# Attention and depthwise convolution on one core: groups of seven steps, one buffer for v, and most statistics of x taken during the first image

## The chip, the cores and the metric

The kernel runs on one core of a Trainium2 chip. The metric is device time in microseconds of one execution, as the median of several runs. The core has TensorE (matmuls, PE in the profile), VectorE (DVE), ScalarE (ACT), GpSimd (POOL) and the queue engine SP, which only issues DMAs here. DMAs are also issued from GpSimd's queue and, in the tail, from ScalarE's.

## The reference

x has 16 images of 384 channels on a 32 x 32 grid, all float32. Two residual layers follow each other:

```python
x = x + attention(_gn(x), w_qkv, w_proj, b_proj)   # 8 heads of 48, 1024 tokens per image
x = x + _dwconv(_gn(x), w_sym)                     # 7 x 7 per channel, padding 3

def _gn(v, G=32, eps=1e-5):      # mean and variance over 12 channels x 1024 points
    g = v.reshape(B_, G, C_ // G, H_, W_)
    ...
attn = softmax((q @ k.T) * 48 ** -0.5)
out = (attn @ v) @ w_proj.T + b_proj
w_sym = (weight + rot90(weight, 1) + rot90(weight, 2) + rot90(weight, 3)) * 0.25
```

## The kernel before

An image is three tiles of 128 channels x 1024 tokens. Its 8 heads are four units of two heads; a unit has two halves of 512 queries, and each half eight steps of 128 keys, so an image has 64 steps. A step is `s_step` (two score matmuls side by side into a PSUM buffer of two banks, L331, then the exp on ScalarE, L339) and `av_step` (the exponentials times v, L347, which also sums the softmax's denominators through a column of ones in v). The PSUM pool `ps_s` has three such buffers, which scores, q/k (`qk_step`, L280), v (`v_step`, L306) and projection (`proj_step`, L398) share; `ps_o` has two banks for the sums of AV. `take` (L358) copies a finished half to SBUF on ScalarE.

The division by the denominators goes through DRAM: `sums_out` (L365, L366) writes them and reads them back spread over partitions, `invert` (L372) takes the reciprocal on VectorE, writes it and reads it back broadcast, `divide` (L383) multiplies. After an image's fourth unit the projection follows, ScalarE adds the bias (L406) and a DMA on GpSimd's queue adds x (L407): this is x1.

Group norm statistics are `Stats`: `channels` (bn_stats on VectorE, L195), `gather` (through DRAM to 32 rows, GpSimd's queue), `groups` (L208 to L220: bn_aggr on VectorE, called mv; then on GpSimd one addition of eps, ve, L210, the power -1/2 and two small operations, L212 to L214; then two DMAs that spread scale and shift, sc, over the channels). Each image has them twice, for x and for x1. For the first image's x and the last image's x1 `groups_on_pe` does the same with small matmuls against masks (L236). `apply` normalizes: x on ScalarE (`x_apply`, L265), x1 into a tile xn on GpSimd (`conv_begin`, L261).

The convolution is 49 taps per tile on VectorE, each one instruction (`conv_tap`, L455) that reads xn and x1 and adds into x1. Three tiles are worked on in turn. Four of the 48 tiles, two of image 14 and two of image 15, are done by TensorE instead (`conv_on_pe`, L557), from shifted copies that go through DRAM; VectorE adds their sum (L570). The output leaves on GpSimd's queue (L465).

Each engine runs its own instructions in the order in which the program lists them. That order comes from a planner in the kernel: it keeps a `clock` for TensorE and a `vclock` for VectorE from cost constants (US_STEP 1.716, US_TURN 0.353 and so on). The main loop takes GS = 4 steps at a time: four S, four AV, then one `project` or some q/k and v chunks of the next image when `credit` allows, then `catch_up`, which lists VectorE's work (taps, and functions that fell due through `after`) until `vclock` reaches `clock`. `finish`, called within the loop, lets the reciprocal fall due 7 us after its call. x of the next image is loaded when the last v chunk is issued (`issue`, `begin_x`), into a single buffer. The last unit of the last image is divided without DRAM (`divide_at_once`, L418 to L421) and projected from four 128-row weight tiles (`proj_part`, L431), of which three fit in `wp`.

Of the kernel before, what the change touches and what calls it, by code (L numbers as in the profile page):

```python
# [16 lines left out]
P = 128  # L17
HEADS = 8
# [26 lines left out]
def kernel(  # L45
# [64 lines left out]
    def run(general):  # L110
        tag = "g" if general else "f"
        with ExitStack() as stack:
# [11 lines left out]
            epool = pool("epool", 6)  # L124
# [14 lines left out]
            PE_TILES = [(b, k) for b in (B - 2, B - 1) for k in PE_K]  # L139
# [25 lines left out]
            nc.sync.dma_start(wp, w_proj_t.rearrange("(k p) c -> p k c", p=P))  # L165
# [7 lines left out]
            vs = []  # L173
            for i in range(2):
                t = wpool.tile([P, NT, VW], F32, name=f"v_{i}")
                nc.gpsimd.memset(t, 1.0)
                vs.append(t)
# [4 lines left out]
            mhalf = wpool.tile([P, NK], F32, name="mhalf")  # L182
# [5 lines left out]
            class Stats:  # L188
# [35 lines left out]
                def groups_on_pe(self, masks):  # L224

                    st = small.tile([P, NK, 2], F32, tag="st", name=f"st_{self.name}")
                    for k in range(NK):
                        nc.vector.bn_aggr(st[:, k, :], self.bs[:, k, :])
                    ps = ps_o.tile([P, HALF], F32, tag="acc", name=f"ps_st_{self.name}")

                    def average(c0, src):
                        for mo in range(NK):
                            blocks = [n for n, b in enumerate(MASK_BLOCKS) if b[1] == mo]
                            for n in blocks:
                                ki = MASK_BLOCKS[n][0]
                                nc.tensor.matmul(  # L236
                                    ps[:, c0 + mo : c0 + mo + 1],
                                    lhsT=masks[:, n, :],
                                    rhs=src[:, ki : ki + 1],
                                    start=(n == blocks[0]),  # L240
                                    stop=(n == blocks[-1]),
                                )

                    mean = small.tile([P, NK], F32, tag="mn", name=f"mn_{self.name}")
                    nc.vector.tensor_copy(mean, st[:, :, 0])
                    average(0, mean)
                    d = small.tile([P, NK], F32, tag="d", name=f"d_{self.name}")
                    nc.vector.tensor_tensor(d, mean, ps[:, 0:NK], ALU.subtract)
                    nc.vector.tensor_tensor(d, d, d, ALU.mult)
                    nc.vector.tensor_tensor(d, d, st[:, :, 1], ALU.add)  # L250
                    average(NK, d)
                    nc.vector.tensor_scalar(d, ps[:, NK : 2 * NK], EPS, None, ALU.add)
                    self.sc = small.tile([P, NK, 2], F32, tag="sc", name=f"sc_{self.name}")
                    nc.gpsimd.tensor_tensor(self.sc[:, :, 0], d, mhalf, ALU.pow)
                    nc.vector.scalar_tensor_tensor(
                        self.sc[:, :, 1], ps[:, 0:NK], -1.0, self.sc[:, :, 0], ALU.mult, ALU.mult
                    )

                def apply(self, dst, src, k, engine=None):
                    if engine is not None:  # L260
                        engine.tensor_scalar(  # L261
                            dst, src, self.sc[:, k, 0:1], self.sc[:, k, 1:2], ALU.mult, ALU.add
                        )
                        return
                    nc.scalar.activation(  # L265
                        dst,
                        src,
                        AF.Identity,
                        bias=self.sc[:, k, 1:2],
                        scale=self.sc[:, k, 0:1],  # L270
                    )

# [28 lines left out]
            def v_step(b, t2):  # L301
# [11 lines left out]
                for j in range(2):  # L313
                    dst = vs[b % 2][:, 2 * t2 + j, 0 : HEADS * (D + 1)]
                    nc.scalar.copy(  # L315
                        dst.rearrange("p (h d) -> p h d", d=D + 1)[:, :, 0:D],
                        ps[:, j, 0:C].rearrange("p (h d) -> p h d", d=D),
                    )

            def v_of(u, i, j):  # L320
                b, p = divmod(u, NP)
                c = (2 * p + j) * (D + 1)
                return vs[b % 2][:, i, c : c + 64]
# [90 lines left out]

            def divide_at_once(u, h):
# [6 lines left out]

            late, pps = {}, {}
# [230 lines left out]
            clock, vclock = 0.0, 0.0  # L654
# [3 lines left out]
            GS = 4  # L658
# [11 lines left out]
            def us_tap(dy, dx):  # L670
                late_us = 0.06 if active[0][0] >= B - 2 else 0.0
                return ((H - abs(dy)) * (W - abs(dx)) + (130 if len(active) > 1 else 270)) / 940 + late_us
# [70 lines left out]
            def x1_groups(b, st):  # L743
                st.groups()
                after(9.0, 0.0, lambda: x1_chains(b, st))

            def x1_chains(b, st):
                on_pe = [t for t in PE_TILES if t[0] == b]
                for k in range(NK - 1, -1, -1):
                    tail = b == B - 1  # L750
                    conv_begin(st, b, k, (nc.gpsimd, None, nc.vector)[k] if tail else nc.gpsimd)
# [9 lines left out]
            def begin_x(b):  # L761
                load_x(b)
                after(10.0, 3.8, lambda: x_channels(b))
# [12 lines left out]
            def x_apply(b, st):  # L776
                for k in range(NK):
                    st.apply(xns[b][:, k, :], xns[b][:, k, :], k)
                ready[b] = now() + 6.0

            def finish(u):
                sums_out(u)
                if u < U - 1:
                    after(7.0, 0.3, lambda: finish2(u))
# [5 lines left out]
            def finish3(u):  # L790
                b, p = divmod(u, NP)
                divide(u)
                if p == NP - 1:
                    proj.append((now() + 4.0, b))

            def queue(b):
                chunks.extend(("qk", b, i) for i in range(4))
                chunks.extend(("v", b, i) for i in range(2))
                chunks.extend(("qk", b, i) for i in range(4, 6))
                chunks.extend(("v", b, i) for i in range(2, 4))  # L800
# [5 lines left out]
            st.groups_on_pe(masks_0.rearrange("p (b c) -> p b c", c=P))  # L806
# [5 lines left out]
            while chunks:  # L812
                issue(chunks.popleft())
            vclock = clock
# [41 lines left out]

            credit = 0.0
            for n0 in range(0, NS, GS):
                b, r = divmod(n0, PER_B)
# [5 lines left out]
                for n in range(n0, n0 + GS):  # L865
                    s_step(n)
                if n0 == NS - 2 * GS:
                    after(3.5, 4.2, lambda: None)
                    divide_at_once(U - 1, 0)
                if n0 == NS - GS:  # L870
                    for o in range(NK):
                        proj_part(B - 1, o, (0, 1))
                    clock += 2 * US_PROJ
                for n in range(n0, n0 + GS):
                    av_step(n)
                    u, h, i = n // (2 * NT), n // NT % 2, n % NT
                    if i == NT - 1:
                        take(u, h)
                        if h == 1:
                            finish(u)  # L880
                clock += GS * US_STEP + US_TURN

                credit = min(credit + 12.0 * GS / PER_B, 2.0)
                if proj and proj[0][0] <= clock:
                    project(proj.popleft()[1])
                elif credit >= 2:
                    while chunks and credit >= 1:
                        kind, cb, i = chunks[0]
                        first = {"qk": 2 * NT * (i // 2), "v": 0, "rest": 2 * NT * 3}[kind]
                        if ready.get(cb, 1e9) > clock or r + GS < first:  # L890
                            break
                        issue(chunks.popleft())
                        credit -= 1
                catch_up(clock)
                if b == 1 and r == 0:
                    conv_prepare()
                if b == B - 1:

                    if r == 4 * GS:
# [3 lines left out]
                    if r == 8 * GS:  # L903
                        w4 = w_proj_4.rearrange("(t p) c -> p t c", p=P)
                        nc.sync.dma_start(wp, w4[:, 0:NK])
                        nc.sync.dma_start(late["w3"], w4[:, NK])
                    if r == 6 * GS:
                        conv_matrices(1, flat2(qkpool.tile([P, 2, N], F32, tag="qk", name="mat_1")))
                    if r == 8 * GS:
# [3 lines left out]
                    if r >= 9 * GS and (b, 0) not in x1s and all(c[0] > b - 2 for c in active):  # L913
# [5 lines left out]
                    if r in (10 * GS, 12 * GS, 14 * GS):  # L919
                        loads(1)  # L920


            late["tail"] = True
            b = B - 1
            divide_at_once(U - 1, 1)
            for t in (NP - 2, NP - 1):
                for o in range(NK):
                    proj_part(b, o, (t,))
            clock += US_PROJ * 4 / 3 + 1.0
            st = Stats(f"x1_{b}")  # L930
            for o in range(NK):
                residual(b, o)
                st.channels(x1s[b, o], o)
            conv_piece()
            st.groups_on_pe(late["masks"])
            clock += 7.0
            x1_chains(b, st)
# [58 lines left out]
```

## Time and profile before

| what | us |
| --- | --- |
| median of 3 runs | 3024.63 (3024.15 to 3026.47) |
| the profiled execution | 3021.88 |
| its span | 3020.0 |
| TensorE busy in it | 2970.3 |
| VectorE busy in it | 2616.1 |
| ScalarE busy in it | 1298.7 |
| GpSimd busy in it | 728.3 |

The profile comes from one execution, and its span begins with the first recorded instruction and ends with the last one. The page gives busy time per engine, the span in 40 slices, the chain of work that ended last, and groups of instructions by line. Starts and durations of single instructions come from the timeline. An idle time in brackets stands before the instruction that it names, with what ended it. The ends of matmuls are modelled, so starts are the safer mark.

### The profile page before, as it was taken

Reading aid. Unit: us, or ns where it says so; the run is one execution under the profiler, and the core shown is the slowest. Engines: PE = TensorE matmul, PEld = TensorE weight load, DVE = VectorE, ACT = ScalarE, POOL = GpSimd, SP = SyncE. Lnnn points to the kernel's source line nnn. Section 1 sums busy time; section 2 is a strip of 40 time slices with the busy share of each in tenths; the row PEclk is TensorE's granted clock in tenths of the full one; section 3 lists DMA queues with packets and bytes.
Section 4 is the critical chain, followed back from the end, with each engine's and each line's share of the span. In section 5 each row is a group of like instructions: output and inputs, shape, how many; then the busy total and the mean of one; then the engine's idle time right before and its main releaser. Section 6 shows DMA issues by size and latency. Waiting matters only on the chain.

```text
span 3020.0 us, 30559 instructions
## 1 busy us (share of the span) xinstructions
PE 2970.3 (98%) x11658; PEld 1166.2 (39%) x11658; DVE 2616.1 (87%) x2553; ACT 1298.7 (43%) x1469; POOL 728.3 (24%) x426
## 2 busy tenths in 40 slices
PE   7999999999999999999999999999999999999978
PEld 4333343433334343343434334343433434333333
DVE  1101898997999999999999999999999999999788
ACT  1534535354453545435353453535445353544400
POOL 1021004020140604215060320505133060411500
PEclk9999999999999999999999999999999999999989
DMA  2113031121312112131211313122131312212234
GB/s 70 38 23 67 15 66 37 39 53 33 67 36 58 23 52 51 36 70 39 52 30 36 66 36 66 42 46 37 36 66 36 66 37 51 37 43 38 89 83 114
DMA packets 68332, 149.42 MB, mean 49 GB/s; under 512 B 30880, under 2 KB 33168, under 8 KB 66640
## 3 DMA queue, kind: packets, MB, share of 16 engines
q1 hardware_dynamic: 47536, 90.80, 12.2%
q0 software_dynamic: 18560, 52.31, 7.8%
q10 hardware_dynamic: 2080, 4.26, 0.6%
q8 instruction: 94, 1.54, 0.2%
q14 instruction: 62, 0.51, 0.1%
HBM read 99.35 MB, written 29.49 MB: 43 GB/s over the span
## 4 chain that ended last, share of the span: by engine, by line
PE 90%; DVE 5%; issue 3%; POOL 1%; DMA 1%; ACT 0%; POOLq 0%; SPq 0%; DVEq 0%
PE ps_s L331 29%; PE acc L347 29%; PE ps_qk L280 16%; PE ps_v L306 8%; PE ps_proj L398 8%; DVE x L455 4%; POOL ve_x L210 1%; DMA wc<-in_w_conv 0%; PE ps_st_x L236 0%; DVE bs_x L195 0%; DMA out<-x 0%; DVE x L570 0%; DMA sums<-sum 0%; DMA sum<-o 0%; DVE o L383 0%
## 5 line engine op out<-in xcount | busy, mean ns | idle before, releaser
L455 DVE SCALAR_TENSOR_TENSOR x<-xn,wsym,x 128x960 f32<-128x960 f32 (+9 forms) x2156 | 2379.2, 1175 | 19.5 <-POOL xn L261 17.6
L339 ACT ACTIVATE e<-ps_s 128x1024 f32<-128x1024 f32 x1024 | 967.0, 1030 | 395.0 <-PE ps_s L331 390.1
L331 PE MATMUL ps_s<-qk 48*128 48x512 f32 x4096 | 948.6, 602 | 2.2 <-ACT e L339 2.2
L347 PE MATMUL acc<-e,v 128*64 128x512 f32 x4096 | 935.4, 598 | 0.0
L331 PEld LDWEIGHTS ps_s<-qk 48*128 48x128 f32 x4096 | 373.1, 186 | 566.8 <-issue 430.6
L347 PEld LDWEIGHTS acc<-e,v 128*64 128x64 f32 x4096 | 271.5, 136 | 632.4 <-issue 561.0
L280 PE MATMUL ps_qk<-x,wqk 128*128 128x512 f32 x1152 | 506.8, 596 | 2.3 <-DVE x L261 2.3
L407 POOL DMA_DIRECT2D x<-in_x x45 | 39.6, 881 | 1414.8 <-ACT x L406 1414.8
L280 PEld LDWEIGHTS ps_qk<-x,wqk 128*128 128x128 f32 x1152 | 217.0, 190 | 284.9 <-issue 278.3
L210 POOL TENSOR_SCALAR ve_x<-mv_x 32x1 f32<-32x1 f32 x30 | 313.8, 10461 | 44.4 <-DVE mv_x L208 43.3
L287 ACT COPY qk<-ps_qk 128x1024 f32<-128x1024 f32 x96 | 97.2, 1012 | 463.4 <-PE ps_qk L280 463.4
L306 PE MATMUL ps_v<-wv,x 128*128 128x384 f32 x768 | 254.5, 488 | 0.0
L398 PE MATMUL ps_proj<-o,wp 128*128 128x512 f32 x540 | 235.7, 595 | 0.2 <-DVE bs_x L195 0.2
L358 ACT COPY o<-acc 128x512 f32<-128x512 f32 x128 | 75.1, 587 | 307.2 <-PE acc L347 307.2
L261 POOL TENSOR_SCALAR xn<-x,sc_x 128x1024 f32<-128x1024 f32 x46 | 198.0, 4309 | 33.5 <-DMA sc_x<-gr_x 33.1
L195 DVE BATCH_NORM_STATS2 bs_x<-x 128x6 f32<-128x512 f32 x192 | 120.2, 680 | 98.8 <-DMA x<-in_x 98.7
L306 PEld LDWEIGHTS ps_v<-wv,x 128*128 128x128 f32 x768 | 144.7, 190 | 113.6 <-issue 20.3
L372 DVE RECIPROCAL rec<-sums 128x16 f32<-128x16 f32 x63 | 15.8, 250 | 185.4 <-DMA sums<-sum 185.3
L398 PEld LDWEIGHTS ps_proj<-o,wp 128*128 128x128 f32 x540 | 101.4, 190 | 134.4 <-issue 131.4
L315 ACT COPY v<-ps_v 128x384 f32<-128x384 f32 x128 | 55.1, 483 | 196.9 <-PE ps_v L306 196.9
L406 ACT ACTIVATE x<-ps_proj,bp 128x1024 f32<-128x1024 f32 x45 | 50.1, 1114 | 192.6 <-PE ps_proj L398 175.0
L383 DVE TENSOR_TENSOR o<-o,inv 128x1024 f32<-128x1024 f32 x63 | 76.6, 1216 | 55.5 <-DMA inv<-inv 34.0
(70 smaller groups left out, 486.1 us busy)
## 6 DMA issues: line engine op xcount, KB each, us to landing
inv<-inv SPq DMA_DIRECT2D x126, 256.0 KB
x<-in_x SPq DMA_DIRECT2D x48, 512.0 KB
x<-in_x POOLq DMA_DIRECT2D x48, 512.0 KB, 5.5
out<-x POOLq DMA_DIRECT2D x48, 512.0 KB, 3.5
qk<-qk SPq DMA_DIRECT2D x96, 128.0 KB
sh<-xd SPq DMA_DIRECT2D x38, 160.0 KB
o<-o SPq DMA_DIRECT2D x90, 64.0 KB
sh<-xd ACTq DMA_DIRECT2D x26, 160.0 KB
```

The costliest lines, as they stand in the source:

```text
L195: nc.vector.bn_stats(self.bs[:, k, 6 * h : 6 * h + 6], src[:, h * HALF : (h + 1) * HALF])
L210: nc.gpsimd.tensor_scalar(ve, mv[:, 1:2], EPS, None, ALU.add)
L261: engine.tensor_scalar(dst, src, self.sc[:, k, 0:1], self.sc[:, k, 1:2], ALU.mult, ALU.add)
L280: nc.tensor.matmul(ps[:, h, :], lhsT=wqk[:, k, s, t, :], rhs=xns[b][:, k, h * HALF : (h + 1) * HALF], start=(k == 0), stop=(k == NK - 1),)
L287: nc.scalar.copy(halves(qks[u][:, s, :]), ps)
L306: nc.tensor.matmul(ps[:, j, 0:C], lhsT=xns[b][:, k, t * P : (t + 1) * P], rhs=wv[:, k, :], start=(k == 0), stop=(k == NK - 1),)
L331: nc.tensor.matmul(ps[:, j, :], lhsT=qks[u][r, 1, i * P : (i + 1) * P], rhs=qks[u][r, 0, h * HALF : (h + 1) * HALF], start=True, stop=True,)
L339: nc.scalar.activation(es[n], ps, AF.Exp, scale=SCALE)
L347: nc.tensor.matmul(accs[u, h][64 * j : 64 * j + 64, :], lhsT=v_of(u, i, j), rhs=e[:, j, :], start=(i == 0), stop=(i == NT - 1),)
L383: nc.vector.tensor_tensor(os_[u], os_[u], invs.pop(u), ALU.mult)
L398: nc.tensor.matmul(ps[:, h, :], lhsT=wp[:, t, o * P : (o + 1) * P], rhs=os_[NP * b + t][:, h * HALF : (h + 1) * HALF], start=(t == 0), sto ...
L455: nc.vector.scalar_tensor_tensor(acc, xn1s[b, k].rearrange("p (h w) -> p h w", w=W)[:, iy, ix], wsym[:, k, dy + PAD, dx + PAD : dx + PAD + 1],
```

## The change

- The main loop takes groups of 7 steps, eight times, and one of 8 (`SIZES`). Chunks, projection and `catch_up` now have a place after the scores of a group too (`other`). The pool of exponentials has 8 buffers, not 6.
- v has one buffer. Its four chunks stand after an image's first group of scores; q/k of the next image are issued during the image as before.
- The statistics of x of images 2 to 15 are taken during the first image: `stream_in` loads each tile once more (42 loads of 512 KB), `stream_stats` takes bn_stats, `stream_gather` and `stream_groups` do all groups at once, into `x_sc`. `x_apply` of these images falls due 14 us after the load of x is issued.
- The first image ends as the last one does (`fast_finish`, `fast_end`): last unit divided without DRAM, four weight tiles, statistics on TensorE. `wp` gets its usual content afterwards.
- `conv_begin` normalizes x1 of images 1 to 14 on ScalarE (engine None) instead of GpSimd; images 0 and 15 use one engine for each tile. It falls due 14 us after `groups`, not 9.
- The reciprocal falls due 9 us after the end of its group.
- Three conv tiles are on TensorE: one of image 14, two of image 15. The planner's price of a tap changes.

```diff
-            epool = pool("epool", 6)
+            epool = pool("epool", 8)
...
-            PE_TILES = [(b, k) for b in (B - 2, B - 1) for k in PE_K]
+            FAST = (0, B - 1)
+            PE_TILES = [(B - 2, PE_K[0])] + [(B - 1, k) for k in PE_K]
...
-            vs = []
-            for i in range(2):
-                t = wpool.tile([P, NT, VW], F32, name=f"v_{i}")
-                nc.gpsimd.memset(t, 1.0)
-                vs.append(t)
+            v = wpool.tile([P, NT, VW], F32, name="v")
+            nc.gpsimd.memset(v, 1.0)
+            x_sc = wpool.tile([P, B, NK, 2], F32, name="x_sc")
...
+            def stream_in(b, k):
+                if not many:
+                    many["bs"] = npool.tile([P, B - 2, NK, 12], F32, tag="xn1", name="bs_all")
+                many[b, k] = rpool.tile([P, N], F32, tag="x1", name=f"xs_{b}_{k}")
+                nc.gpsimd.dma_start(
+                    many[b, k], x[b, k * P : (k + 1) * P].rearrange("p h w -> p (h w)")
+                )
+
+            def stream_stats(b, k):
+                t = many.pop((b, k))
+                for h in range(2):
+                    nc.vector.bn_stats(
+                        many["bs"][:, b - 2, k, 6 * h : 6 * h + 6], t[:, h * HALF : (h + 1) * HALF]
+                    )
...
-            GS = 4
+
+            SIZES = [7] * 8 + [8]
...
-                after(9.0, 0.0, lambda: x1_chains(b, st))
+                after(14.0, 0.0, lambda: x1_chains(b, st))
...
-                    tail = b == B - 1
-                    conv_begin(st, b, k, (nc.gpsimd, None, nc.vector)[k] if tail else nc.gpsimd)
+                    conv_begin(st, b, k, (nc.gpsimd, None, nc.vector)[k] if b in (0, B - 1) else None)
...
-                after(10.0, 3.8, lambda: x_channels(b))
+                if b == 1:
+                    after(10.0, 3.8, lambda: x_channels(b))
+                else:
+                    after(14.0, 0.0, lambda: x_apply(b, None))
...
-                if u < U - 1:
-                    after(7.0, 0.3, lambda: finish2(u))
+                if u % NP < NP - 1 or u // NP not in FAST:
+                    waiting.add(u)
+                    after(9.0, 0.3, lambda: finish2(u))
...
+            def fast_finish(b):
+                nonlocal clock, vclock
+                late["tail"] = b == B - 1
+                proj_part(b, 0, (NP - 2,))
+                divide_at_once(NP * b + NP - 1, 1)
+                for o in range(1, NK):
+                    proj_part(b, o, (NP - 2,))
+                x1_stats[b] = Stats(f"x1_{b}")
+                for o in range(NK):
+                    proj_part(b, o, (NP - 1,))
+                    residual(b, o)
+                    x1_stats[b].channels(x1s[b, o], o)
...
-                for n in range(n0, n0 + GS):
+                for n in range(n0, n0 + size):
                     s_step(n)
...
+                clock += (size * US_STEP + US_TURN) / 2
+                if r == 0 and b - 1 == FAST[0]:
+                    fast_end(b - 1)
+                if r == 0:
+                    for i in range(NT // 2):
+                        issue(("v", b, i))
...
+                else:
+                    other(r + size)
...
-                clock += GS * US_STEP + US_TURN
+                clock += (size * US_STEP + US_TURN) / 2
+                if n0 // (2 * NT) < (n0 + size) // (2 * NT):
+                    finish((n0 + size) // (2 * NT) - 1)
```

## Prediction

> **What bounds the kernel now.** I read the page first: busy times, then the chain that ended last.
>
> ```profile
> PE 2970.3 (98%) x11658; PEld 1166.2 (39%) x11658; DVE 2616.1 (87%) x2553; ACT 1298.7 (43%) x1469; POOL 728.3 (24%) x426
> ...
> DVE  1101898997999999999999999999999999999788
> ...
> PE 90%; DVE 5%; issue 3%; POOL 1%; DMA 1%; ACT 0%; POOLq 0%; SPq 0%; DVEq 0%
> ```
>
> TensorE carries the end. VectorE is nearly idle for four slices (300 us) and full afterwards; ScalarE is never on the chain. Next the chain in order of time (start, us, what): one projection per image.
>
> ```profile
> 53.81 10.30 PE ps_qk L280 x24
> ...
> 1498.12 15.65 PE ps_proj L398 x36
> ...
> 1676.24 15.65 PE ps_proj L398 x36
> ```
>
> An image takes 178.12 us, without TensorE idling. 24 full matmul passes take 10.30, so 0.429 each; a step (scores S, then AV) is 16 passes that run in pairs, 8 x 0.429 = 3.43 per group of 4 on each side. The timeline of one group, TensorE and then ScalarE (start, us, engine, line):
>
> ```profile
> 1691.82 3.70 PE L331 MATMUL ps_s<-qk 48*128 48x512 f32 x16
> 1695.45 3.65 PE L347 MATMUL acc<-e,v 128*64 128x512 f32 x16
> 1699.04 3.70 PE L331 MATMUL ps_s<-qk 48*128 48x512 f32 x16
> ```
>
> ```profile
> 1691.93 1.11 ACT L406 ACTIVATE x<-ps_proj,bp 128x1024 f32<-128x1024 f32 x1 [4.04 <-PE ps_proj L398]
> 1693.06 3.77 ACT L339 ACTIVATE e<-ps_s 128x1024 f32<-128x1024 f32 x4
> ...
> 1700.27 3.77 ACT L339 ACTIVATE e<-ps_s 128x1024 f32<-128x1024 f32 x4 [3.44 <-PE ps_s L331]
> ```
>
> S to AV is 3.63, AV to S 3.59: a group costs 7.22, of which 7.22 - 6.87 = 0.355 is the turn. The first exp starts 1.24 after its group (1693.06 - 1691.82), right behind the projection's copy; four exps take 3.77, so 0.91 from start to start and 1.03 each.
>
> Where ScalarE normalizes x today, and what GpSimd's small operations wait for (ScalarE, GpSimd, VectorE):
>
> ```profile
> 1558.25 3.77 ACT L339 ACTIVATE e<-ps_s 128x1024 f32<-128x1024 f32 x4 [0.53 <-PE ps_s L331]
> 1561.88 3.52 ACT L265 ACTIVATE x<-x,sc_x 128x1024 f32<-128x1024 f32 x3
> 1565.47 3.77 ACT L339 ACTIVATE e<-ps_s 128x1024 f32<-128x1024 f32 x4
> ```
>
> ```profile
> 1539.46 19.98 POOL L210 TENSOR_SCALAR ve_x<-mv_x 32x1 f32<-32x1 f32 x1
> ...
> 1569.30 11.57 POOL L261 TENSOR_SCALAR xn<-x,sc_x 128x1024 f32<-128x1024 f32 x1 [1.58 <-DMA sc_x<-gr_x]
> ```
>
> ```profile
> 1560.84 0.25 DVE L372 RECIPROCAL rec<-sums 128x16 f32<-128x16 f32 x1 [1.48 <-DMA sums<-sum]
> ```
>
> The three x operations sit behind four exps, in the AV half, and the next exps start on time (1558.25 + 7.22 = 1565.47). The 32x1 operation on GpSimd lasts 19.98 us and ends at 1559.44, when VectorE falls idle (1559.36 to 1560.84). Last, the clock in the tail (stretch, PE busy, ..., PEclk):
>
> ```profile
> 2870.00:2876.00 6.00, 4.10 (x18) 1.16 (x14) 5.86 (x5) 0.58 (x1) 0.00 (x0) 1.00 1.04 235
> 2876.00:2880.00 4.00, 2.13 (x4) 0.83 (x3) 3.96 (x4) 0.00 (x0) 0.00 (x0) 0.61 0.30 66
> 2880.00:2884.00 4.00, 4.00 (x6) 1.59 (x5) 3.89 (x4) 0.00 (x0) 0.00 (x0) 0.53 0.00 0
> ```
>
> Two idle stretches of 1.90 and 1.87 us (TensorE's timeline, before 2875.34 and 2878.31) halve the clock for the busy stretch behind them: its matmuls follow each other at 0.853.
>
> **What the Trainium skill says.** "PSUM — Partial Sum Buffer", section "Engine vs sequencer instructions": ScalarE's queue is a strict FIFO. The trace agrees (the first exp waits for the 1.11 us copy). "SBUF — State Buffer", section "Who interferes with whom": a VectorE operation with two SBUF inputs contends with a GpSimd one that reads SBUF. Taps are such; the 19.98 us agree. "TensorE: Matmul & The Clock Gate", section "What's actually happening": half clock after an idle window of 3.4 us, full after a busy one. The trace is harsher: PEclk 0.53 after shorter idling.
>
> **The change part by part.** From the order in which the changed kernel's instructions stand on each engine.
>
> *Groups of seven.* 16 groups per image become 9: 7 x 0.355 = 2.49 less, and one insertion more (+0.2, as 10.50 against 10.30): 175.8 per image. Three PSUM buffers let S run 3 steps ahead of its exp. Step 7 begins at 5.25 and needs exp 4, done at 1.24 + 3 x 0.91 + 1.03 = 5.0: it just fits, if ScalarE is free at the start. v in one buffer moves 15.7 us of matmuls behind an image's first S: no cost, AV of the last image is over.
>
> *x normalized at another place.* For images 3 to 15 the three x operations stand on ScalarE behind the projection's third copy and before the next seven exps (13 times). The first exp then starts at 1.24 + 3.57 = 4.81; S step 4 waits until 5.9 instead of 2.67, the seventh is 3.4 late. +3.4 each, nothing hides it. TensorE idles 3.2 us: half clock costs 0 to 3.4 more; I take 1.4, since the idling may be cut by a window's edge.
>
> *xn moved from GpSimd to ScalarE* (images 1 to 13): three more operations behind a pair of q/k copies and before seven exps, the same +3.4 at least. They wait for GpSimd's statistics, which nobody but GpSimd waited for. Between VectorE's mv and the first tap of the new image stand 31 taps, two reciprocals and a divide, and no wait that could bring a gap: the sums are now asked for 9 us after the group instead of 7 after its start. So I take it that the 32x1 operation is released only when VectorE runs dry before that tap. Bounds: 0 (released at once) to the following walk. From the first exp after xn: S ends 4.7; AV 6.15, S 6.2, AV 6.15, S 6.2, q/k 10.5, AV 6.15, S8 7.05, AV8 7.0 = 60.1; S 6.2, v 15.8, AV, S, AV 18.5, projection 15.65 = 116.3. Third x1 in place +7.2 (copy 1.2, GpSimd's DMA 5.5), bn_stats 1.2, 13 taps 14.2, mv 0.7, 31 taps and the rest 34.3: 173.9. Then from the end of ve to sc 9.9 (1559.44 to 1569.30), 0.1, xn 3.6: 187.5; half clock after 6 us of idling 2.6 (0 to 3.4). Period **190.1** instead of 178.12, with TensorE alone at 186.6 inside it. Image 2 is spared (VectorE idle): 175.8 + 9.6. In image 15 xn stands in the AV half of group 6, 160.6 after the same mark, and waits longer: mv at 124.7 + 9 taps 9.7 + conv matrices 2.2 + 0.7 = 137.3; 23 taps, matrices, a divide and reciprocals 28.0; 11 taps 11.8, where VectorE runs dry, since the inverse that it needs next stands on SP's queue behind the store of xn; then 10.0 and 3.6: 190.7. The next exps were due at 166.5: +24.2, and 5 for two half clocks.
>
> *First image.* Projection over four tiles (+5.2), two ones-matmuls (2), a wait for the 3.35 us reciprocal (1), statistics on TensorE 5 (as 2911.57 to 2916.58) and half clock 2. 42 loads of 512 KB every 4 us and their bn_stats (1.29 a pair) lie in VectorE's idle slices, where the DMA engines are 1 to 3 tenths busy. On GpSimd's queue they stand ahead of image 1's own statistics, needed on ScalarE at about 146 and done by 112. That the scales of 14 images come late for image 2: 0 to 10, I take 0.
>
> *Three conv tiles.* TensorE's tail loses 94.8/4 = 23.7, but VectorE's grows: after the last statistics 119 taps stand where 73 stood, since image 14's two tiles start no earlier. Before: 2918.06 to 3009.39 = 91.3; 46 taps at 1.08 less one addition: **138**. VectorE then ends last, 47 us over before, and the 23.7 are worth nothing.
>
> **Sum.** First q/k at 23.7, +32.5; image 0: 113.0 (64 x 1.716 + 9 x 0.355) + v 15.7 + a pair of q/k 10.5 + projection of two units 10.5, of the others 10.3 and 3.0 for ones-matmuls and the reciprocal; four q/k 21: image 1 starts at 240.2. +113 + 7 + 15.7 + 31.8 = 407.7, image 2. First exp after its xn: +123.7 = 531.4. 12 x 190.1: 2812.6. Image 15: S8, AV8 and the partial projection end 47.6 after 190.7, +5: 3055.9. To the last statistics 24.6 (as before, without its wait), +138.9, +10.6 to the end: span 3230. The profiled execution took 3021.88 for a span of 3020.0, the median is 3024.63: +4.6, so **3235**.
>
> **Rivals.**
> B, GpSimd gets through in time (xn was once let in two taps after a divide; no ve was): period 175.8 + 2 x 4.8 = 185.4, image 15 without the wait: 2756 + 217 + 174 + 4.6 = **3151**.
> C, not slower: ScalarE's queue never reaches TensorE. Its place is the 27 lumps, its price 0 instead of 3.4 and more; it decides if the seven exps start within 0.2 us of before. For it: ScalarE is 43% busy and off the chain. Against it: FIFO and three PSUM buffers. 407.7 + 13 x 175.8 + 155 (image 15: 113 + v 15.7 + two projections 26.2) + 174 + 4.6 = **3027**, no change; somewhat below 3018 if VectorE, no longer disturbed by GpSimd's xn (taps of 1.95 us), runs the tail quicker.
> D, more stalls (late scales, 3.4 for each half clock): **3275**.
>
> **Numbers.** A 0.55, B 0.27, C 0.10, D 0.08. The range takes A, B and most of D: 3115 to 3275. 0.2% (6 us) is what a measurement of this kernel tells from no change: slower 0.91, same 0.04, faster 0.05, the last two out of C.
>
> **What would show it.** Projections 190 us apart from image 2 on (178.12 before, 175.8 under C); on L331 idle time put down to ACT, near 3 us behind the projection; ve of GpSimd 30 us long, ending where VectorE idles; PEclk below 9; a tail in which VectorE works 138 us. If S groups take 6.2 everywhere, the prediction is wrong at the lumps.

## The result and the profile after

The changed kernel takes 3249.73 us (median of 4 runs, 3246.39 to 3251.95), the kernel before 3025.55 beside it: a ratio of 1.074, 95% interval 1.0722 to 1.0759. The profiled execution has a span of 3247.2 us.

The page, read in the same order as before: busy times, VectorE and TensorE's clock in 40 slices, and the first line of the chain that ended last.

```profile
PE 2992.1 (92%) x11478; PEld 1198.7 (37%) x11478; DVE 2645.5 (81%) x2608; ACT 1336.4 (41%) x1509; POOL 646.6 (20%) x317
...
DVE  3438933889989888998888989888898988899688
...
PEclk9999999999999999999999999999999999999895
...
DVE 4%; issue 1%; POOL 0%; POOLq 0%
```

TensorE's share fell from 98% to 92%, so it now waits. The prediction's sign "PEclk below 9" hardly shows: the digits stay at 9 except in two of the last three slices, each an average over 81 us. The mean granted clock over the whole execution does show it, 0.954 against 0.994 before. The chain covers only 5% of the span: it begins at 3096.93 us, at the last statistics, and could not be followed back further. It shows who ended last, and nothing of where 224 us went. For that one compares periods and groups of instructions. Two groups say most (busy us, mean ns of one, then the idle time before them and its releaser):

```profile
L401 PE MATMUL ps_s<-qk 48*128 48x512 f32 x4096 | 988.9, 632 | 152.7 <-ACT e L409 152.7
L217 POOL TENSOR_SCALAR ve_x<-mv_x 32x1 f32<-32x1 f32 x15 | 446.5, 29766 | 151.6 <-DVE mv_x L215 151.6
```

The score matmuls S idle 152.7 us, all put down to the exps of ScalarE. An addition on 32 numbers takes GpSimd 29.8 us on average. Of its 15 executions 13 take 33.86 to 39.55 us and two, at 96.13 and 485.12, take 0.25; during the one at 485.12 VectorE has nothing to do. TensorE's timeline of one image in the middle shows where the waits stand (start, length, ..., in brackets the idle time before):

```profile
1595.93 15.72 PE L468 MATMUL ps_proj<-o,wp 128*128 128x512 f32 x36
1611.58 2.85 PE L401 MATMUL ps_s<-qk 48*128 48x512 f32 x12
1617.15 5.45 PE L401 MATMUL ps_s<-qk 48*128 48x512 f32 x16 [2.73 <-ACT e L409]
1622.53 10.57 PE L350 MATMUL ps_qk<-x,wqk 128*128 128x512 f32 x24
...
1674.43 2.85 PE L401 MATMUL ps_s<-qk 48*128 48x512 f32 x12
1685.03 6.15 PE L401 MATMUL ps_s<-qk 48*128 48x512 f32 x16 [7.76 <-ACT e L409]
1691.11 6.23 PE L417 MATMUL acc<-e,v 128*64 128x512 f32 x28
```

A group of seven score steps without a wait takes 6.21. The one behind the projection takes 1622.53 - 1611.58 = 10.95, the one behind the q/k pair 1691.11 - 1674.43 = 16.68. In both, three steps (12 matmuls) go through, as many as there are PSUM buffers, and the fourth waits for an exp. From this projection to the next, at 1787.00, lie 191.07 us: 175.85 (the period measured below, in a run without these waits) + 4.74 + 10.47, what the two groups take beyond 6.21. ScalarE in the same stretch:

```profile
1611.69 1.11 ACT L476 ACTIVATE x<-ps_proj,bp 128x1024 f32<-128x1024 f32 x1 [4.04 <-PE ps_proj L468]
1612.70 3.49 ACT L272 ACTIVATE x<-x,x_sc 128x1024 f32<-128x1024 f32 x3
1616.10 3.74 ACT L409 ACTIVATE e<-ps_s 128x1024 f32<-128x1024 f32 x4
...
1674.53 1.01 ACT L357 COPY qk<-ps_qk 128x1024 f32<-128x1024 f32 x1 [4.13 <-PE ps_qk L350]
1680.57 3.50 ACT L272 ACTIVATE xn<-x,sc_x 128x1024 f32<-128x1024 f32 x3 [5.03 <-DMA sc_x<-gr_x]
1683.98 2.82 ACT L409 ACTIVATE e<-ps_s 128x1024 f32<-128x1024 f32 x3
```

The first exp starts 4.52 after its scores where x stands in front, and 9.55 where xn does, since xn waits 5.03 more for its scales. What these wait for is on GpSimd, and what releases GpSimd is on VectorE (first GpSimd's timeline, then VectorE's):

```profile
1637.59 33.87 POOL L217 TENSOR_SCALAR ve_x<-mv_x 32x1 f32<-32x1 f32 x1 [10.46 <-DVE mv_x L215]
```

```profile
1669.37 2.00 DVE L524 SCALAR_TENSOR_TENSOR x<-xn,wsym,x 128x841 f32<-128x841 f32 x2
1684.11 3.67 DVE L524 SCALAR_TENSOR_TENSOR x<-xn,wsym,x 128x1024 f32<-128x1024 f32 x3 [12.74 <-ACT xn L272]
```

The addition ends at 1671.46, 0.1 after VectorE's last tap (1671.37), and VectorE then waits for the xn whose scales that addition held up. So the loop is closed. At the end, VectorE's timeline from the last image's normalization to its last taps:

```profile
3097.16 0.81 DVE L268 TENSOR_SCALAR xn<-x,sc_x 128x1024 f32<-128x1024 f32 x1
...
3173.26 63.01 DVE L524 SCALAR_TENSOR_TENSOR x<-xn,wsym,x 128x930 f32<-128x930 f32 x57
```

From 3097.16 to 3236.27 VectorE works 139.1 us, where it worked 91.3 before.

### The profile page after: what moved, and what is told of

Read it like the earlier page. It is cut to its first block, busy times and chain, and to the rows that moved or that the text cites. A ratio compares the mean times of both kernels' runs of the same rounds, so it can differ in the third digit from the quotient of the medians.

```text
span 3247.2 us, 30093 instructions
## 1 busy us (share of the span) xinstructions
PE 2992.1 (92%) x11478; PEld 1198.7 (37%) x11478; DVE 2645.5 (81%) x2608; ACT 1336.4 (41%) x1509; POOL 646.6 (20%) x317
## 3 DMA queue, kind: packets, MB, share of 16 engines
q1 hardware_dynamic: 46800, 88.82, 11.1%
## 5 line engine op out<-in xcount | busy, mean ns | idle before, releaser
L524 DVE SCALAR_TENSOR_TENSOR x<-xn,wsym,x 128x899 f32<-128x899 f32 (+9 forms) x2205 | 2402.4, 1166 | 165.3 <-ACT xn L272 163.9
L401 PE MATMUL ps_s<-qk 48*128 48x512 f32 x4096 | 988.9, 632 | 152.7 <-ACT e L409 152.7
L417 PE MATMUL acc<-e,v 128*64 128x512 f32 x4096 | 910.7, 596 | 0.0
L401 PEld LDWEIGHTS ps_s<-qk 48*128 48x128 f32 x4096 | 399.0, 197 | 733.3 <-ACT e L409 389.4
L417 PEld LDWEIGHTS acc<-e,v 128*64 128x64 f32 x4096 | 281.2, 137 | 609.4 <-issue 609.4
L217 POOL TENSOR_SCALAR ve_x<-mv_x 32x1 f32<-32x1 f32 x15 | 446.5, 29766 | 151.6 <-DVE mv_x L215 151.6
L468 PE MATMUL ps_proj<-o,wp 128*128 128x512 f32 x504 | 220.0, 595 | 0.0
L468 PEld LDWEIGHTS ps_proj<-o,wp 128*128 128x128 f32 x504 | 94.6, 190 | 125.2 <-issue 123.3
L385 ACT COPY v<-ps_v 128x384 f32<-128x384 f32 x128 | 55.1, 483 | 186.6 <-PE ps_v L376 186.6
L202 DVE BATCH_NORM_STATS2 bs_x<-x 128x6 f32<-128x512 f32 x108 | 69.2, 687 | 64.8 <-DMA x<-in_x 64.5
L272 ACT ACTIVATE xn<-x,sc_x 128x1024 f32<-128x1024 f32 x44 | 51.5, 1231 | 105.2 <-DMA sc_x<-gr_x 77.4
```

Source lines behind the costliest of these rows:

```text
L202: nc.vector.bn_stats(self.bs[:, k, 6 * h : 6 * h + 6], src[:, h * HALF : (h + 1) * HALF])
L217: nc.gpsimd.tensor_scalar(ve, mv[:, 1:2], EPS, None, ALU.add)
L401: nc.tensor.matmul(ps[:, j, :], lhsT=qks[u][r, 1, i * P : (i + 1) * P], rhs=qks[u][r, 0, h * HALF : (h + 1) * HALF], start=True, stop=True,)
L417: nc.tensor.matmul(accs[u, h][64 * j : 64 * j + 64, :], lhsT=v_of(u, i, j), rhs=e[:, j, :], start=(i == 0), stop=(i == NT - 1),)
L468: nc.tensor.matmul(ps[:, h, :], lhsT=wp[:, t, o * P : (o + 1) * P], rhs=os_[NP * b + t][:, h * HALF : (h + 1) * HALF], start=(t == 0), sto ...
L524: nc.vector.scalar_tensor_tensor(acc, xn1s[b, k].rearrange("p (h w) -> p h w", w=W)[:, iy, ix], wsym[:, k, dy + PAD, dx + PAD : dx + PAD + 1],
```

## The experiments

Each is the changed kernel with the edit shown; times are medians, and ratios are to the kernel before, run beside them. None leaves out any of the computation.

**Statistics without starvation, the order kept**

```diff
-                    nc.gpsimd.tensor_scalar(ve, mv[:, 1:2], EPS, None, ALU.add)
+                    nc.vector.tensor_scalar(ve, mv[:, 1:2], EPS, None, ALU.add)
...
-                    nc.gpsimd.tensor_tensor(af[:, 1:2], mv[:, 0:1], af[:, 0:1], ALU.mult)
-                    nc.gpsimd.tensor_scalar(af[:, 1:2], af[:, 1:2], -1.0, None, ALU.mult)
+                    nc.vector.scalar_tensor_tensor(
+                        af[:, 1:2], mv[:, 0:1], -1.0, af[:, 0:1], ALU.mult, ALU.mult
+                    )
```

> The changed kernel, where in the images without a wait of VectorE for statistics (the groups of one image) the variance + eps goes to VectorE, and behind GpSimd's power the product -mean*rstd too: VectorE has to wait for GpSimd here, so that the power runs in a gap of VectorE's, 34 us earlier than now. The order of everything else stays. Theory (GpSimd is starved by the taps until VectorE runs dry, the scales reach ScalarE late, and in a FIFO the seven exps wait behind them): the 34 us are gone, xn costs what a lump of 3.6 us costs in any case (4.75 as behind the projection), the period falls from 191 to about 185.4, image 15 loses its wait of 24 us and more; 3249.7 - 12 x 5.6 - 27 = about 3155 (3140 to 3170). Rival (the scales are late for another reason, such as the place where the statistics are asked for, and the 34 us only fill the wait): 3250, period 191.

Measured: 3153.05, ratio 1.0424 (1.0406 to 1.0442). From 453.53 to 2865.59, the starts of the projections of images 1 and 14, lie 13 periods of 185.5 each. The theory's 3155 and 185.4 hold: the lateness of the scales is worth 96.7 us.

**The same with the addition left on GpSimd**

Only the second half of the diff above.

> The changed kernel with variance + eps and the power left on GpSimd, as one edit only: the product -mean*rstd is taken on VectorE, which so waits for GpSimd right behind its mv. Nothing else on GpSimd or ScalarE changes. Theory (GpSimd's 32x1 operation is starved by VectorE's taps and runs at once where VectorE waits): the operation lasts under 1 us instead of 34, and the time falls as with the variance on VectorE, to about 3153 (3145 to 3165). Rival (the operation is long or late of itself on GpSimd, so that VectorE now waits for it too): 3250 or more, since VectorE's taps of 34 us then stand behind it.

Measured: 3156.41, ratio 1.0441 (1.0424 to 1.0459). The addition's group of instructions:

```profile
L217 POOL TENSOR_SCALAR ve_x<-mv_x 32x1 f32<-32x1 f32 x15 | 3.4, 226 | 153.9 <-DVE mv_x L215 153.9
```

The same instruction on the same engine takes 226 ns instead of 29766, because VectorE stands still beside it: in the image with the addition at 1603.03, VectorE waits 1.00 us for GpSimd before its product. The addition was starved, not slow: this run shows it.

**xn back on GpSimd, which is starved as it was**

```diff
-                    conv_begin(st, b, k, (nc.gpsimd, None, nc.vector)[k] if b in (0, B - 1) else None)
+                    conv_begin(st, b, k, (nc.gpsimd, None, nc.vector)[k] if b in (0, B - 1) else nc.gpsimd)
```

> The changed kernel with one part undone: xn of every image but the first and last is computed by GpSimd again, not by ScalarE; GpSimd's statistics are starved as before. Theory (the wait costs only because ScalarE's queue carries it to TensorE): the S groups behind the q/k pair take 6.2 again, only the lump of x behind the projection stays (4.75), the period is 175.8 + 4.8 = 180.6, image 15 loses its 24 us and more: 3249.7 - 12 x 10.4 - 27 = about 3098 (3085 to 3115). Rival (VectorE is then late: dry 10 us for the scales and 11.6 more for GpSimd's xn, and its divides stand behind the taps that wait): 155 busy + 22 dry is near the period already, TensorE then waits for the divides and the time stays above 3130.

Measured: 3122.36, ratio 1.032 (1.0303 to 1.0338), between the two. The addition still takes 29.8 us on average, yet S behind q/k takes 6.21 again: late scales cost TensorE through ScalarE's queue. The period is 181.4 rather than 180.6, since S behind the projection takes 11.85 to 12.38 in four of 13 images; in eight others it takes 10.9 to 11.1, in the first 9.36. The other miss is in the last image, in TensorE's timeline:

```profile
2935.66 3.78 PE L500 MATMUL ps_proj<-o,wp 128*128 128x512 f32 x4 [9.42 <-DVE o L453]
```

VectorE's divides are late there, and a further wait of 6.87 follows. These two waits (16.3) and 0.8 in each of 12 periods (9.6) are about the 24 us by which the theory missed. So the rival was right for the last image only.

**x alone moved into the AV half, statistics starved**

A function put in `mid` is called right after the scores of a group and behind their exps.

```diff
+            mid = deque()
...
-                    after(14.0, 0.0, lambda: x_apply(b, None))
+                    after(14.0, 0.0, lambda: mid.append(lambda: x_apply(b, None)))
...
+                    while mid:
+                        mid.popleft()()
```

> The changed kernel, GpSimd's starved statistics left as they are, and only x's three operations moved from before the seven exps into the AV half behind them. The order that is worked out from costs shifts with it: xn's three now stand behind a group's exps and a q/k pair, in the AV half as well, about 64 us of TensorE's work behind the projection, and 32 taps instead of 44 stand between the last x1 and the point where VectorE runs dry. Theory (starvation has no price of its own; what counts is when the scales come against where xn stands, and whether exps follow at once): xn is ready at 7.2 + 1.2 + 10.9 + 0.7 + 27 + 10 + 3.6 = 60.6 behind the projection, before the AV half ends at about 70; so no stall although the 32x1 operation still lasts 20 us and more: period near 175.9, and with 6 taps more in the tail and a possible wait in image 15 3020 to 3060, about 3035. Rival (each stall has its own price, and starvation keeps its own): 3249.7 - 13 x 4.75 = 3188, period 186.

Measured: 3277.58, ratio 1.0839 (1.0822 to 1.0855). Both missed. I had worked out the order of one image and taken it for all, but the planner's order repeats only after three images here: projections stand 175.9, 206.2 and 201.6 apart. xn on ScalarE in an image of the first kind and in one of the second:

```profile
1695.56 3.50 ACT L272 ACTIVATE xn<-x,sc_x 128x1024 f32<-128x1024 f32 x3 [0.36 <-DMA sc_x<-gr_x]
...
1878.94 3.50 ACT L272 ACTIVATE xn<-x,sc_x 128x1024 f32<-128x1024 f32 x3 [27.57 <-DMA sc_x<-gr_x]
```

GpSimd's addition in the same two:

```profile
1662.02 24.03 POOL L217 TENSOR_SCALAR ve_x<-mv_x 32x1 f32<-32x1 f32 x1 [17.66 <-DVE mv_x L215]
...
1827.33 43.66 POOL L217 TENSOR_SCALAR ve_x<-mv_x 32x1 f32<-32x1 f32 x1 [8.31 <-DVE mv_x L215]
```

In the first kind it goes as the theory had it: 24 us of starvation, no stall, a period of 175.87. In the two others xn stands some 20 us earlier against the projection, in front of seven exps, and that group of scores takes 36.6 and 31.9 instead of 6.2. An edit that took away a stall of 4.75 per image moved another instruction to a place where it costs 25 to 30.

**The same order, statistics not starved**

The first diff and the one above together.

> The kernel with x's three operations in the AV half (the one at 3277.6) with the one addition that VectorE takes variance + eps and the product, so that GpSimd isn't starved. The order is the same as there: in one image of three xn stands in the AV half, in the two others some 20 us earlier, behind an AV and before seven exps. Theory (a lump in front of exps costs 4.75, and the 25 to 30 us more that those images took were the wait for starved scales): xn there finds its scales, since they come some 27 to 30 us behind the projection and it stands 40 behind it; periods 175.9, 180.6, 180.6, and 3020 + 9 x 4.75 + 9 taps x 1.08 = about 3073 (3060 to 3085). Rival (xn's early place itself is what makes it wait, starved or not): still above 3200.

Measured: 3030.52, ratio 1.0021 (1.0014 to 1.0028). In this order starvation alone is worth 3277.6 - 3030.5 = 247 us. The rival is out, and the theory missed by 42.5: I had priced an xn before the exps at 4.75, and it costs 0.08 (that S group takes 6.29). With 0.08 in its place the theory's sum is 3030. ScalarE's timeline of it:

```profile
1915.08 3.50 ACT L273 ACTIVATE xn<-x,sc_x 128x1024 f32<-128x1024 f32 x3
1918.49 1.91 ACT L410 ACTIVATE e<-ps_s 128x1024 f32<-128x1024 f32 x2
```

Its scores begin at 1917.05. xn starts 2 us earlier, because no copy stands before it that has to wait until TensorE turns to the scores, and the first exp comes 1.44 after them. So, as far as these runs show, what three operations cost depends on what holds their start: the copy of a projection or of q/k, or a late scale.

**Both sets of three in the AV half, statistics not starved**

To the run before is added:

```diff
-                after(14.0, 0.0, lambda: x1_chains(b, st))
+                after(14.0, 0.0, lambda: mid.append(lambda: x1_chains(b, st)))
```

> The changed kernel with the statistics of an image on VectorE as in the run without starvation, and both sets of three ScalarE operations (x behind the projection, xn behind q/k) put behind the exps of an S group, into the AV half, where ScalarE is idle. All work is the same, and three conv tiles stay. Theory (a lump costs by its place, in front of seven exps): no S group above 6.3 behind the projection or q/k, period 175.8, and the late scales of image 2 stay (+9.6): about 3033 (3022 to 3045), which is where the changed kernel would have been without any stall of ScalarE's. Rival (groups of seven leave ScalarE too little room, exps late anyway, or VectorE's waits come to bind): period above 180, more than 3085.

Measured: 3020.04, ratio 0.9989 (0.998 to 0.9998). The scores' group, which had 152.7 us of idle time:

```profile
L402 PE MATMUL ps_s<-qk 48*128 48x512 f32 x4096 | 918.7, 597 | 0.5 <-ACT e L410 0.5
```

Projections stand 175.85 apart. The time is 2 us under the theory's range: the late scales of image 2, for which it kept 9.6, cost TensorE nothing once x stands in the AV half. Against 3153.05 the 27 sets of three are worth 133.0, or 4.9 on average. One of the 27 is image 2's x, whose S group there takes 13.65 (7.4 more than 6.21) because of the late scales.

**Four conv tiles, in the changed kernel and in the one without stalls**

```diff
-            PE_TILES = [(B - 2, PE_K[0])] + [(B - 1, k) for k in PE_K]
+            PE_TILES = [(b, k) for b in (B - 2, B - 1) for k in PE_K]
```

> The changed kernel with one part undone: four conv tiles on TensorE at the end, not three. Theory (VectorE ends last, its 119 taps behind the last statistics set the end): 46 taps of 1.08 less and one addition of 1.2 more, VectorE's tail 139 -> about 91, TensorE's tail 23.7 longer but still not behind it: about 3202 (3195 to 3210). Rival (TensorE's conv tail was the longer or close behind, so that its 23.7 come back): 3225 or more.

> The kernel without stalls of ScalarE (statistics on VectorE, both lumps in the AV half), with four conv tiles on TensorE as in the kernel before. Theory (the two cuts add up, since they lie one behind the other): 3020.0 - 45 taps x 1.08 + one addition = about 2973, or a little later where TensorE's conv tail (95 us from the statistics on) ends after VectorE's: 2970 to 2985, 1.3 to 1.8% under the kernel before. Rival (TensorE's tail then binds by its full 23.7): 2995 or more.

Measured: 3199.44, ratio 1.0582 (1.0565 to 1.06), and 2974.03, ratio 0.9834 (0.982 to 0.9847). Three tiles for four cost 50.3 us in one kernel and 46.0 in the other, and the 23.7 that they spare TensorE do not show. In the second kernel both engines end together (TensorE's last conv matmuls, then VectorE's last addition):

```profile
2912.46 46.70 PE L627 MATMUL ps_conv<-sh,mat 128*32 128x512 f32 x452
```

```profile
2959.35 1.22 DVE L640 TENSOR_TENSOR x<-ps_conv,x 128x1024 f32<-128x1024 f32 x1
```

TensorE is busy for 99% of this span. It is the fastest version of the study, 1.7% under the kernel before.

**Groups of four in that version**

```diff
-            SIZES = [7] * 8 + [8]
+            SIZES = [4] * 16
```

> The kernel without stalls and with four conv tiles on TensorE, but in 16 groups of four steps an image instead of 9 of seven and eight: what the longer groups alone are worth. Theory (each turn between S and AV costs 0.355, less one insertion): period 178.1 instead of 175.85, 16 x 2.3 = 37 more than the groups of seven: about 3012 (3005 to 3020). Rival (the turns overlap with other work, or three steps of lead make short groups cheaper): within 10 of the groups of seven.

Measured: 3020.63, ratio 0.9988 (0.9981 to 0.9994), just above the theory's range and far from the rival's. The period is 178.4, so groups of seven save 2.55 per image, about 41 us in 16. The other 6 stand in the tail, where the conv on TensorE waits 3.73 and 2.34 for its shifted copies.

## Why the prediction came out

From the kernel before to the changed one the runs make a ladder:

| version | us | step |
| --- | --- | --- |
| before | 3023.8 | |
| the other parts of the change: groups of four, four tiles, no stalls | 3020.6 | -3 |
| groups of seven | 2974.0 | -47 |
| three conv tiles | 3020.0 | +46 |
| x and xn on ScalarE, in front of exps | 3153.1 | +133 |
| scales late through starvation: the change as made | 3249.7 | +97 |

The likeliest case, A, is what happened, and the time lies in the range. By its steps:

- *Groups of seven.* Predicted 2.3 less per image, measured 2.55. That seven steps just fit ScalarE holds: S groups of 6.21 wherever nothing stands in front.
- *x at another place.* Predicted 4.8 (3.4, and 1.4 for the clock), measured 4.74. That the sum fits so closely is partly luck. Where the clock stays full (last section) the same group takes 9.37, so the wait itself costs 3.16, not 3.4; the clock's part is then 1.6 here, and between 0 and 3 in other runs. The reason given for it, that a window's edge may cut the idling, agrees with what that section reads from the trace.
- *xn on ScalarE.* Predicted period 190.1. The first exps after xn in images 2 and 14 lie (2830.1 - 538.3)/12 = 191.0 apart. The addition lasts 33.87 as its median and is released where VectorE runs dry, at the place which the walk had named. The 0.9 are VectorE's: it runs dry 59.7 after the projection's end, not 57.6, while from the addition's end to xn it takes 9.1, not 10. Image 15 loses 24.06 (its S group lasts from 2998.64 to 3028.91): TensorE waits 21.13, and 2.9 go to the lower clock behind it (0.57). Predicted were 24.2 for the wait and 5 for the clock.
- *The Trainium skill's statements* that carried this step hold. "SBUF — State Buffer", section "Who interferes with whom", has the contention of GpSimd with VectorE's two-input operations; the runs show that the addition is held up beside VectorE's work and give it a size here, 226 ns against 29766. No run isolates what the two engines share as the cause. The strict FIFO of "PSUM — Partial Sum Buffer", section "Engine vs sequencer instructions", is what carries it to TensorE: S behind q/k takes 16.68 with xn on ScalarE and 6.21 with it on GpSimd.
- *First image.* Image 1's first scores start at 239.53 (predicted 240.2). The term that was mis-sized is "That the scales of 14 images come late for image 2: 0 to 10, I take 0": x waits 8.85 on ScalarE for `x_sc`, and the S group at 285.56 takes 15.80, which is 9.6 more.
- *Tail.* The sum has 138.9 for VectorE from the last statistics, measured 139.1, and 10.9 for 10.6 from there to the end. The prediction's own terms (91.3, and 46 taps at 1.08 less one addition of 1.2) give 139.8, not the 138 that it prints.

The span is 17 us above the 3230 of the sum: 6.9 at the mark of image 2, which are the late scales less smaller terms, and 10.7 in twelve periods (0.3 less after them). From the span to the median it was 2.5, not 4.6.

The two faster rivals were right about their own mechanism. B (3151) is what the changed kernel takes when GpSimd gets through in time: 3153. C (3027) is what it takes when ScalarE never holds TensorE: 3020. C's "tail quicker" did not come: 139 us.

Open stays which of the smaller parts of the change (first image without DRAM, early statistics of x, v in one buffer) pay for themselves. With the order that comes with them they are worth -3 together, and they were not taken apart.

## What to carry to other kernels

When work moves to an engine that is idle on average, look up what stands behind it in that engine's queue and what it waits for itself: here 3.5 us of work on an engine that was 43% busy cost TensorE 0.1, 4.7, 10 or 30 us by its place and its inputs. A small operation may be slow without harm until its result is put in front of critical work; before doing that, ask what it shares with its neighbours. And where a planner makes the order, read a whole cycle of it, since removing one stall can move another instruction.

## What was not expected of the hardware

A stall of one length can cost different times. In the run with the addition left on GpSimd, three S groups behind x (the first two) or xn (the third), in the view of stretches (stretch, its length and PE's busy time, ..., then granted clock, DMA share and GB/s):

```profile
1576.98:1586.36 9.38, 6.66 (x30) 2.29 (x29) 9.38 (x11) 9.27 (x10) 0.85 (x1) 1.00 0.47 79
1759.06:1769.96 10.90, 8.18 (x29) 3.20 (x29) 10.90 (x13) 9.85 (x10) 0.85 (x1) 0.84 0.40 70
...
1453.20:1465.44 12.24, 9.61 (x30) 3.62 (x29) 7.69 (x7) 10.21 (x10) 0.00 (x0) 0.72 0.29 99
```

TensorE idled 2.72, 2.73 and 2.63 us in them. The clock stayed full in the first; the other two paid 1.5 and 2.9 us more for slower matmuls. The periods of this kernel alternate between 182.1 and 186.6 in most images.

What decides can be read from the clock in the same trace. It is granted in full or at half, and all its changes lie, within 0.01 us, on one grid of steps of 3.413 us; during the stalls it is half for one step or for two. The third stall above, cut at this grid in the same view:

```profile
1454.78:1458.19 3.41, 1.26 (x6) 0.20 (x3) 0.44 (x1) 3.41 (x4) 0.00 (x0) 1.00 0.57 210
1458.19:1461.61 3.42, 2.94 (x8) 1.40 (x10) 3.42 (x4) 3.01 (x4) 0.00 (x0) 0.50 0.00 0
1461.61:1465.02 3.41, 3.41 (x10) 1.15 (x8) 3.41 (x4) 2.04 (x3) 0.00 (x0) 0.50 0.00 0
1465.02:1468.43 3.41, 3.41 (x16) 1.05 (x16) 3.41 (x4) 1.30 (x2) 0.00 (x0) 1.00 0.00 0
```

So an idle time counts by how the grid cuts it:

| idling starts, length | TensorE idle in the two steps that it touches | granted clock behind it | that S group |
| --- | --- | --- | --- |
| 1579.83, 2.72 | 1.24 and 1.48 | full | 9.37 |
| 1761.90, 2.73 | 0.08 and 2.65 | half for one step | 10.90 |
| 1456.04, 2.63 | 2.15 and 0.48 | half for two steps | 12.24 |

This run has 26 stalls of 2.6 to 2.7 us. All 12 that put more than 2.1 us of idling into one step are followed by half clock; of the 14 with at most 1.54 us in either step only one is. Two periods together, 368.65, are 108 steps, so every second image meets the grid at the same place, and the alternation keeps itself up. This is a reading of the trace afterwards: no run shifted a stall against the grid on purpose.
